# First block ahead, first loads reordered, router logits in four column groups: one order string for another

## The chip, the core and the metric

The kernel runs on one core of one Trainium2 chip. The metric is the device time of one execution in microseconds (us), as a median of runs. A core has a matmul engine (PE, or TensorE, with its weight loads shown apart as PEld), a vector engine (DVE), an activation engine (ACT) and a general-purpose engine (POOL). Each takes its instructions in program order. SP issues most of the DMA transfers, and ACT issues a few at the start. Matmuls write to PSUM, which DVE and ACT then read.

## What is computed

The input x has 4 batches of 1024 tokens with 128 features, all in float32. The work is one pre-norm block, cut here to what matters:

```
xn      = layernorm(x)
Q, K, V = silu(xn @ Wq), silu(xn @ Wk), silu(xn @ Wv)     # 8 heads of 16
scores  = (Q K^T + rel_bias[i - j]) / 4, causal, keys that are all zero masked
attn    = silu(scores) V                                   # silu, not softmax
x       = x + attn * silu(xn @ Wu)
x2      = layernorm(x)
logits  = x2 @ w_gate^T                                    # 8 experts
gates   = softmax over the two largest logits, 0 elsewhere
out     = x + sum_e gates[e] * ((x2 @ w_in[e]^T) @ w_out[e]^T)
```

## The kernel before, in words

**Tiling.** A batch has two blocks of 512 tokens, and a block has four tiles of 128 tokens. `prepare(b, blk)` (L289) makes one block's projections: a layer norm with four transposes onto the PE (L283), a copy to SBUF (L284), K (L304, with ACT writing two half-masked copies of it, one for even and one for odd heads, L307), Q (L312, L313), the key mask (DVE compares the two K copies, L318; four small matmuls, L323; L328), V (L334, L339, and POOL's L341, which writes the masked values `vp`) and U (L351, L352).

**Attention.** `attend` (L355) takes a group of query tiles: groups 0 to 6 are whole blocks, and the last block is split in two groups of two tiles. A group consists of units. A unit is up to 512 score columns for the four heads of one parity. The PE writes them into four PSUM banks (L425), DVE adds the bias from the table `near` (L444) or ACT reads the banks directly where the bias is constant (L452), ACT applies the silu (L447), and one step later the PE weighs the values with the result (L403). When a group is done, DVE multiplies by U (L412) and queues `finish`.

**Router and experts.** `finish` (L470) adds the residual, makes the second layer norm, computes the router logits (L494, copied out by DVE at L496), chooses the top two with a chain of some fifteen small DVE operations and one POOL power (L520), and for groups 0 to 6 sends the gates through DRAM to all partitions (L542 to L547), where DVE multiplies them into the tokens (L553). `experts` (L561) then sums over the experts on the PE (L567). Here w_in and w_out of each expert have been folded into one 128x128 matrix beforehand (`fold`, L242, PE work at L248). The last two groups use `experts_then_gates` (L576): expert products first (L585), gates applied afterwards on ACT (L593) and DVE (L595), then POOL (L599, L600) and DVE (L601).

**What sets the order.** Every one of these functions is a generator that yields between steps, and the string ORDER (L41) says which lane takes its next step: P and Q prepare block 0 and block 1 of each batch, S is one attention unit's scores, W weighs the oldest unit, C, D and E are `finish` of groups 0, 1, 2 modulo 3, X, Y and Z their experts, G the fold, K the constants (the bias table's diagonal and far parts, L193, and clearing `vp`), H the warm-up (L234: four matmuls of the identity with itself, read by nobody). The scheduler doesn't reorder: the letters are the program order of every engine. The string begins:

```
"HHHPPPQQKKKPQPPQQKPQSQKSGGSWSWSG..."
```

All PSUM results except the attention sums share a ring of seven banks (RING, L33, `misc`, L83). A unit takes four of them. So a step waits for the reader of the bank that it reuses.

**First loads.** SP issues x of block 0 and block 1 of batch 0 (L101, L102), the two parities of the bias table `near` (L110), the extended table `ext` to DRAM and from it the two far parts of `near` (L122, L124), then x of batch 1 and the expert weights (L145). ACT issues the bias `rb`, the four projection weights (L107), `cfar` (L131: 1024 elements of 4 bytes) and the gate weights `wgT` (L135).

Of the kernel before, what the change touches and what calls it, by code (L numbers as in the profile page):

```python
# [8 lines left out]
F32 = mybir.dt.float32  # L9
BF16 = mybir.dt.bfloat16  # L10
AF = mybir.ActivationFunctionType
# [5 lines left out]
P = 128  # L17
H = 8
# [5 lines left out]
SB = 512  # L24
TPB = SB // P
E = 8
HID = 512
EPS = 1e-5
NEG = -4294967295.0
# [1 line left out]
OFF = -3.0e38  # L31
EULER = 2.718281828459045
RING = 7  # L33
LAST = 2


# [2 lines left out]


ORDER = (  # L41
    "HHHPPPQQKKKPQPPQQKPQSQKSGGSWSWSGPWPSWWSCPWCSSQWWSCPSQCCPSCWCWPCSCCCWSQGSCWWKCSPPPSWSWSWWCS"
    "WGPSWSWDQSWWSDPGQCWSQQPGQPCCSWSDEQECPPWSQPDSWDWSEGDQEDEDESDWWEDSWQEDSWEWDSXDSWESXSWSWWDSXQ"
    "SEWWSECXECPSWSDEWDWSQPSWDWWDSQYSWWSEEYQPPCSCDSDWCCCESCEWWWCSYQCDSCWSCQYDDCSWWCDWPPQSWSEZQE"
    "SWWSZDCQDSCWDSZCDZCEDDSWDSEEEDWEWSXCSWWCESEWSWSEDDDEXDEXEXDCWDEWSYDCDCCCSCDCCDYCSWDWDCEDDS"
    "CYEYCDSDEEWDWWWDZEEEYYZEZEYEEEEZEYCECCECEEYZYZZZZXZXXX"
)


# [1 line left out]
def preln_silu_attention_moe(  # L51
# [13 lines left out]
    nc = tc.nc  # L65
    B, S, D = x.shape
    NR = rel_biasT.shape[1]
# [15 lines left out]
    def misc():  # L83

        return ps_s.tile([P, SB], F32, tag="bank", name="bank")


    xs = [xpool.tile([P, NT, D], F32, tag="x", name=f"x{b}") for b in range(B)]

# [9 lines left out]
    NPAD = MAXLEN - 1 + TAB  # L99
    FAR = TAB - MAXLEN  # L100
    load_x(0, 0)  # L101
    load_x(0, 1)  # L102
    rb = cpool.tile([H, NPAD], F32, tag="rb", name="rb")
    nc.scalar.dma_start(rb[:, NPAD - NR :], rel_biasT)
    wcat = cpool.tile([P, 4, D], F32, tag="wcat", name="wcat")
    for i, w in ((1, wk), (0, wq), (2, wv), (3, wu)):
        nc.scalar.dma_start(wcat[:, i, :], w)  # L107
    near = cpool.tile([P, 2, NQ, TAB + P], F32, tag="near", name="near")
    for par in range(2):
        nc.sync.dma_start(  # L110
# [3 lines left out]
                [[1, P], [2 * NR, NQ], [1, MAXLEN]],  # L114
            ),
        )
    nc.vector.tensor_copy(
        rb[:, : NPAD - NR], rb[:, NPAD - NR : NPAD - NR + 1].to_broadcast([H, NPAD - NR])
    )
    gates_d = dpool.tile([B * NB, E, SB], F32, tag="gates_d", name="gates_d")  # L120
    ext = dpool.tile([H, NPAD], F32, tag="ext", name="ext")
    nc.sync.dma_start(ext[:, :], rb)  # L122
    for par in range(2):
        nc.sync.dma_start(  # L124
            near[:, par, :, FAR - P : FAR],
            bass.AP(
                ext.tensor, ext.offset + par * NPAD + FAR - P, [[1, P], [2 * NPAD, NQ], [1, P]]
            ),
        )
    cfar = cpool.tile([P, H], F32, tag="cfar", name="cfar")  # L130
    nc.scalar.dma_start(  # L131
        cfar, bass.AP(rel_biasT.tensor, rel_biasT.offset, [[0, P], [NR, H]])
    )
    wgT = cpool.tile([P, E], F32, tag="wgT", name="wgT")
    nc.scalar.dma_start(wgT, w_gateT)  # L135
    experts_in = []
    for e0 in range(0, E, 2):
        if e0 in (0, 4):
            load_x(1, e0 // 4)

        if e0 % 4 == 0:
            room = gpool.tile([P, 2, 2, 2, NC, D], F32, tag="wide", name=f"w_in_out_{e0}")
        both = room[:, e0 // 2 % 2]
        for t, w in zip((both[:, 0], both[:, 1]), (w_in, w_outT)):
            nc.sync.dma_start(t, w[e0 : e0 + 2].rearrange("e (c p) d -> p e c d", p=P))  # L145
        experts_in.append(both)
    for n in range(2 * NB, B * NB):
        load_x(n // NB, n % NB)

    def near_of(k, parts):  # L150

# [81 lines left out]

    def warm():  # L234

        for _ in range(3):
            pt = misc()
            for i in range(TPB):
                nc.tensor.matmul(pt[:, i * P : (i + 1) * P], ident, ident, start=True, stop=True)
            yield  # L240

    def fold():  # L242

        for e0, both in zip(range(0, E, 2), experts_in):
            for e in range(2):
                pt = misc()
                for c in range(NC):
                    nc.tensor.matmul(  # L248
                        pt[:, :D], both[:, 0, e, c, :], both[:, 1, e, c, :],
                        start=(c == 0), stop=(c == NC - 1),  # L250
                    )
                nc.scalar.copy(wfold[:, e0 + e, :], pt[:, :D])
                yield
# [35 lines left out]
    def prepare(b, blk):  # L289

        if b not in batches:
            batches[b] = {
                "qT": bpool.tile([P, S], F32, tag="qT", name=f"qT{b}"),
                "kT": bpool.tile([P, 2, S], F32, tag="kT", name=f"kT{b}"),
                "uT": bpool.tile([P, S], F32, tag="uT", name=f"uT{b}"),
                "vp": vps[b % 2],
            }
        qT, kT, uT, vp = (batches[b][n] for n in ("qT", "kT", "uT", "vp"))
        t0 = blk * TPB
        s0 = blk * SB  # L300
        xnT = spool.tile([P, SB], F32, tag="xnT", name="xnT")
        yield from layernorm_T(xs[b][:, t0 : t0 + TPB, :], xnT, "ACT", (b, blk) == (0, 0))
        pt = misc()
        nc.tensor.matmul(pt, wcat[:, 1, :], xnT, start=True, stop=True)  # L304

        for par in range(2):
            nc.scalar.activation(  # L307
                kT[:, par, s0 : s0 + SB], pt, AF.Silu, scale=sel[:, par : par + 1]
            )
        yield  # L310
        pt = misc()
        nc.tensor.matmul(pt, wcat[:, 0, :], xnT, start=True, stop=True)  # L312
        nc.scalar.activation(qT[:, s0 : s0 + SB], pt, AF.Silu)  # L313
        yield


        nz = spool.tile([P, SB], BF16, tag="nz", name="nz")
        nc.vector.tensor_tensor(  # L318
            nz, kT[:, 0, s0 : s0 + SB], kT[:, 1, s0 : s0 + SB], ALU.not_equal
        )  # L320
        pt = misc()
        for i in range(TPB):
            nc.tensor.matmul(  # L323
                pt[:, i * H : (i + 1) * H], nz[:, i * P : (i + 1) * P], ones8,
                start=True, stop=True,
            )
        kmask = spool.tile([P, TPB, H], F32, tag="kmask", name="kmask")
        nc.vector.tensor_scalar(  # L328
            kmask.rearrange("p i h -> p (i h)"), pt[:, : TPB * H], 0.0, None, ALU.not_equal
        )  # L330
        yield
        pt = misc()
        for i in range(TPB):
            nc.tensor.matmul(  # L334
                pt[:, i * P : (i + 1) * P], xnT[:, i * P : (i + 1) * P], wcat[:, 2, :],
                start=True, stop=True,
            )
        v = spool.tile([P, TPB, D], F32, tag="v", name="v")
        nc.scalar.activation(v.rearrange("p i d -> p (i d)"), pt, AF.Silu)  # L339
        for par in range(2):  # L340
            nc.gpsimd.tensor_tensor(  # L341
                vp[:, t0 : t0 + TPB, par, :, par, :],
                v.rearrange("p i (k q c) -> p i k q c", k=NQ, q=2)[:, :, :, par, :],
                kmask.rearrange("p i (k q) -> p i k q", q=2)[:, :, :, par]
                .unsqueeze(3)
                .to_broadcast([P, TPB, NQ, HD]),
                ALU.mult,
            )
        yield
        pt = misc()  # L350
        nc.tensor.matmul(pt, wcat[:, 3, :], xnT, start=True, stop=True)  # L351
        nc.scalar.activation(uT[:, s0 : s0 + SB], pt, AF.Silu)  # L352
        yield

# [115 lines left out]
    def finish(g, b, t0, nt, gated):  # L470
# [18 lines left out]

        xT = spool.tile([P, nt, P], F32, tag=f"x2T{nt}", name="x2T")  # L490
        yield from layernorm_T(x2, xT.rearrange("p i t -> p (i t)"), "DVE", nt < TPB)
        pt = misc()
        for i in range(nt):
            nc.tensor.matmul(pt[:, i * E : (i + 1) * E], xT[:, i, :], wgT, start=True, stop=True)  # L494
        lg = eight("lg")
        nc.vector.tensor_copy(lg, pt[:, : nt * E].rearrange("p (i e) -> p i e", e=E))  # L496
        yield

        def first_of_largest(v, m, oh, k):
# [61 lines left out]
    def experts(b, t0, gated):  # L561

        y = spool.tile([P, TPB, D], F32, tag="y", name="y")
        for i in range(TPB):
            pt = misc()
            for e in range(E):
                nc.tensor.matmul(  # L567
                    pt[:, :D], gated[:, e, i * P : (i + 1) * P], wfold[:, e, :],
                    start=(e == 0), stop=(e == E - 1),
                )  # L570
            nc.vector.tensor_tensor(y[:, i, :], pt[:, :D], xs[b][:, t0 + i, :], ALU.add)  # L571
            if i == TPB - 1:
                store(b, t0, TPB, y)
            yield

    def experts_then_gates(b, t0, nt, xT, gates):  # L576
# [3 lines left out]
        for i in range(nt):  # L580
            one = xs[b][:, t0 + i, :]
            gy = spool.tile([P, EH, D], F32, tag="gy", name="gy")
            for e0 in (EH, 0):
                pt = misc()
                nc.tensor.matmul(  # L585
                    pt, xT[:, i, :], wfold[:, e0 : e0 + EH, :].rearrange("p e d -> p (e d)"),
                    start=True, stop=True,
                )
                for e in range(EH):
                    ye = pt[:, e * D : (e + 1) * D]  # L590
# [83 lines left out]
```

## Time and profile before

| | us |
|---|---|
| median of three runs | 291.55 (291.19 to 292.44) |
| the profiled execution | 292.34 |
| its span, first to last instruction | 290.2 |
| PE busy / DVE / ACT / POOL | 278.4 / 228.5 / 198.9 / 102.1 |
| first score matmul (L425) starts | 20.96 |
| last expert matmul (L567) ends in the chain of waits | 282.06 |

The span is 2.1 us shorter than the time of the same execution. An engine's busy time is the union of its instructions. Since matmuls are pipelined, and their ends are modelled, a busy PE says only that something was in it. The distance from one matmul's start to the next one's start, which the timeline gives, says more. A float32 matmul stands in the trace as two passes (two instructions), so 32 router matmuls are "x64". A transpose is one pass.

### The profile page before, as it was taken

The numbers are of one execution on the slowest core, as the hardware profiler recorded it, in microseconds if no ns is written. First come the engines' busy times: TensorE is split into PE (matmuls) and PEld (weight loads), VectorE is DVE, ScalarE is ACT, GpSimd is POOL, SyncE is SP. The second block draws the span as 40 slices with busy tenths as digits, with TensorE's granted clock in tenths as the row PEclk, the third lists the DMA queues.
The fourth block names the chain that finished last, engine by engine and source line by source line (L and its number), as shares of the span: only waits on it lengthen the run. The fifth ranks groups of instructions, "written<-read, shape, count | busy, mean of one in ns | idle before, by whom it ended". The sixth has DMA issues, their size and how long they took to land.

```text
span 290.2 us, 6505 instructions
## 1 busy us (share of the span) xinstructions
PE 278.4 (96%) x2591; PEld 161.4 (56%) x2591; DVE 228.5 (79%) x571; ACT 198.9 (69%) x327; POOL 102.1 (35%) x126
## 2 busy tenths in 40 slices
PE   8599999999999999999999999999999999999993
PEld 8255434344445445355653463666676687787873
DVE  4148957688998876879878979887999887797794
ACT  1166899899879779778789787775686683472120
POOL 3913079033306868101125347101601162102251
PEclk9779999999999999999999999999999999999999
DMA  6999100000070000000444300016001702617102
GB/s 190 267 312 317 44 3 1 2 0 3 2 291 0 2 0 3 0 3 0 167 165 145 150 0 0 2 38 273 20 1 40 291 5 75 255 33 296 40 0 72
DMA packets 22061, 25.47 MB, mean 88 GB/s; under 512 B 1952, under 2 KB 21128, under 8 KB 21136
## 3 DMA queue, kind: packets, MB, share of 16 engines
q1 hardware_dynamic: 20256, 24.78, 24.6%
q10 hardware_dynamic: 1776, 0.29, 0.6%
q8 instruction: 20, 0.33, 0.5%
q14 instruction: 9, 0.07, 0.1%
HBM read 22.83 MB, written 2.24 MB: 86 GB/s over the span
## 4 chain that ended last, share of the span: by engine, by line
PE 54%; issue 17%; POOL 17%; DVE 7%; ACT 2%; DMA 1%; POOLq 0%; DVEq 0%
PE bank L425 14%; PE bank L567 14%; PE av L403 12%; POOL xn L276 11%; DVE w L444 5%; POOL rstd L271 4%; PE bank L585 2%; PE bank L494 2%; PE bank L304 2%; PE bank L312 2%; POOL vp L341 2%; PE bank L334 2%; PE bank L283 2%; DMA x<-in_L_attn_x 1%; PE bank L351 1%
## 5 line engine op out<-in xcount | busy, mean ns | idle before, releaser
L444 DVE TENSOR_TENSOR w<-bank,near 128x512 f32<-128x512 f32 (+2 forms) x220 | 116.4, 591 | 22.2 <-PE bank L425 18.7
L447 ACT ACTIVATE w<-w 128x1024 f32<-128x1024 f32 (+2 forms) x110 | 98.4, 913 | 35.7 <-DVE w L444 32.5
L425 PE MATMUL bank<-qT,kT 32*128 32x512 f32 (+3 forms) x864 | 85.6, 481 | 0.0
L452 ACT ACTIVATE w<-bank,cscaled 128x512 f32<-128x512 f32 (+3 forms) x136 | 69.6, 597 | 12.5 <-PE bank L425 12.4
L403 PE MATMUL av<-w,vp 128*32 128x512 f32 (+3 forms) x864 | 71.9, 456 | 0.0
L567 PEld LDWEIGHTS bank<-wfold,gated 128*128 128x128 f32 x448 | 51.9, 192 | 8.1 <-DVE w L444 2.4
L425 PEld LDWEIGHTS bank<-qT,kT 32*128 32x128 f32 x864 | 36.2, 184 | 36.1 <-issue 13.0
L567 PE MATMUL bank<-wfold,gated 128*128 128x128 f32 x448 | 55.1, 279 | 0.0
L276 POOL TENSOR_SCALAR xn<-x,st,rstd 128x128 f32<-128x128 f32 x59 | 52.2, 896 | 1.8
L271 POOL TENSOR_TENSOR rstd<-rs,mhalf 128x4 f32<-128x4 f32 (+1 forms) x17 | 19.0, 1118 | 78.6 <-DVE rs L267 60.5
L403 PEld LDWEIGHTS av<-w,vp 128*32 128x32 f32 x864 | 22.5, 109 | 39.8 <-issue 31.1
L553 DVE TENSOR_TENSOR gated<-gated,x2T 128x1024 f32<-128x1024 f32 x28 | 34.5, 1254 | 0.0
L520 POOL TENSOR_TENSOR ex<-euler,d 128x4 f32<-128x4 f32 (+1 forms) x9 | 10.8, 1199 | 52.8 <-DVE d L518 47.7
L341 POOL TENSOR_TENSOR vp<-v,kmask 128x256 f32<-128x256 f32 x16 | 9.7, 630 | 44.5 <-ACT v L339 44.5
L283 PE MATMUL bank<-ident,xn 128*128 128x128 f32 x64 | 12.8, 299 | 5.8 <-POOL xn L276 5.7
L593 ACT ACTIVATE gy<-bank,gates 128x128 f32<-128x128 f32 x16 | 4.6, 368 | 16.7 <-PE bank L585 10.7
L283 PEld LDWEIGHTS bank<-ident,xn 128*128 128x128 f32 x64 | 8.1, 148 | 11.5 <-POOL xn L276 8.6
L262 DVE BATCH_NORM_STATS2 st<-x 128x6 f32<-128x256 f32 x32 | 12.2, 420 | 0.8 <-DMA x<-in_L_attn_x 0.5
L307 ACT ACTIVATE kT<-bank,sel 128x512 f32<-128x512 f32 x16 | 10.2, 704 | 1.6 <-PE bank L304 1.6
L571 DVE TENSOR_TENSOR y<-bank,x 128x128 f32<-128x128 f32 x28 | 7.8, 284 | 2.9 <-PE bank L567 2.9
L304 PE MATMUL bank<-xnT,wcat 128*128 128x512 f32 x16 | 10.1, 729 | 0.0
L248 PEld LDWEIGHTS bank<-w_in_out 128*128 128x128 f32 x64 | 7.9, 191 | 2.7 <-issue 1.0
(77 smaller groups left out, 211.5 us busy)
## 6 DMA issues: line engine op xcount, KB each, us to landing
gated<-gates_d SPq DMA_DIRECT2D x7, 2048.0 KB, 7.1
x<-in_L_attn_x SPq DMA_DIRECT2D x8, 256.0 KB, 4.2
w_in_out<-in_L_ffn_w_in SPq DMA_DIRECT2D x4, 512.0 KB, 6.2
w_in_out<-in_L_ffn_w_out SPq DMA_DIRECT2D x4, 512.0 KB, 6.3
out<-y SPq DMA_DIRECT2D x7, 256.0 KB, 2.4
near<-in_L_attn_rel_bias SPq DMA_DIRECT2D x2, 512.0 KB, 6.4
near<-ext SPq DMA_DIRECT2D x2, 256.0 KB, 5.3
out<-y SPq DMA_DIRECT2D x2, 128.0 KB, 1.9
```

Of the source, the lines that this page charges most:

```text
L271: nc.gpsimd.tensor_tensor(rstd[:, :nt], rs[:, :nt], mhalf[:, :nt], ALU.pow)
L276: (nc.vector if quick and i != 1 else nc.gpsimd).tensor_scalar(xn[:, i, :], src[:, i, :], st[:, i, 1:2], rstd[:, i : i + 1], ALU.subtract, ...
L283: nc.tensor.transpose(pt[:, i * P : (i + 1) * P], xn[:, i, :], ident)
L304: nc.tensor.matmul(pt, wcat[:, 1, :], xnT, start=True, stop=True)
L341: nc.gpsimd.tensor_tensor(vp[:, t0 : t0 + TPB, par, :, par, :], v.rearrange("p i (k q c) -> p i k q c", k=NQ, q=2)[:, :, :, par, :], kmask ...
L403: nc.tensor.matmul(acc[k * 32 : (k + 1) * 32, nt * P - n : nt * P], vp[:, j, par, k, :, :].rearrange("p q c -> p (q c)"), w[:, k, c : c + ...
L425: nc.tensor.matmul(ps[k][:, c : c + n], kT[k * 32 : (k + 1) * 32, par, j * P : (j + 1) * P], qT[k * 32 : (k + 1) * 32, lo : lo + n], start ...
L444: nc.vector.tensor_tensor(w[:, k, :nn], ps[k][:, :nn], near_of(k, parts), ALU.add)
L447: nc.scalar.activation(w[:, k : k + 2, :nn], w[:, k : k + 2, :nn], AF.Silu, scale=SCALE)
L452: nc.scalar.activation(w[:, k, lo:hi], ps[k][:, lo:hi], AF.Silu, bias=cscaled[:, h : h + 1], scale=SCALE,)
L553: nc.vector.tensor_tensor(wide_g[:, e0 : e0 + 2, :], wide_g[:, e0 : e0 + 2, :], xT.rearrange("p i t -> p (i t)").unsqueeze(1).to_broadcast ...
L567: nc.tensor.matmul(pt[:, :D], gated[:, e, i * P : (i + 1) * P], wfold[:, e, :], start=(e == 0), stop=(e == E - 1),)
```

## The change

The warm-up loop gets a constant HEAT, which is 3 as before, and most PE matmuls go through a helper `product`, so that they all carry its line (L90 in the changed kernel). Beyond that:

- **Order string.** It begins with two steps of block 0, constants, and only then a warm-up step. Block 1's first step comes after the key mask of block 0. The second warm-up step lies further on, among the first scores of batch 1, and the third is the last letter of the string.
- **prepare.** The second K copy is written after Q's copy; before, both came ahead of Q.
- **Loads.** x of block 1 goes behind the first parity of `near`, x of batch 1 block 0 behind the second; `cfar` goes ahead of Wq, Wv and Wu on ACT's queue, and the remaining x loads are spread between the expert weights.
- **Router, groups of four tiles.** `wgT` is padded with zeros from 8 to 32 columns (GW) and becomes the stationary operand. Four matmuls write tile i's logits to partitions 32i to 32i+31, so that each uses one column group of the PE. ACT copies the 128x128 result to SBUF, and one transpose brings it back with tokens on partitions. There is a step boundary between the copy and the transpose. Groups of two tiles keep the old form with 32 columns in place of 8.

```
-    load_x(0, 1)
...
-    for i, w in ((1, wk), (0, wq), (2, wv), (3, wu)):
+    nc.scalar.dma_start(wcat[:, 1, :], wk)
...
+    for i, w in ((0, wq), (2, wv), (3, wu)):
         nc.scalar.dma_start(wcat[:, i, :], w)
+    wgT = cpool.tile([P, GW], F32, tag="wgT", name="wgT")
+    nc.gpsimd.memset(wgT, 0.0)
+    nc.scalar.dma_start(wgT[:, :E], w_gateT)
...
+        load_x(par, 1 - par)
...
+        pk = misc()
+        product(pk, wcat[:, 1, :], xnT)
+        keys(0)
+        yield
+        pt = misc()
+        product(pt, wcat[:, 0, :], xnT)
         nc.scalar.activation(qT[:, s0 : s0 + SB], pt, AF.Silu)
+        keys(1)
         yield
...
+        pt = misc()
+        if nt == TPB:
+            for i in range(nt):
+                nc.tensor.matmul(
+                    pt[i * GW : (i + 1) * GW, :P], wgT, xT[:, i, :], start=True, stop=True
+                )
+            across = spool.tile([P, P], F32, tag="across", name="across")
+            nc.scalar.copy(across, pt[:, :P])
+            yield
+            pt = misc()
+            nc.tensor.transpose(pt[:, :P], across, ident)
+        else:
+            for i in range(nt):
+                product(pt[:, i * GW : (i + 1) * GW], xT[:, i, :], wgT)
         lg = eight("lg")
-        nc.vector.tensor_copy(lg, pt[:, : nt * E].rearrange("p (i e) -> p i e", e=E))
+        nc.vector.tensor_copy(
+            lg, pt[:, : nt * GW].rearrange("p (i e) -> p i e", e=GW)[:, :, :E]
+        )
...
 ORDER = (
-    "HHHPPPQQKKKPQPPQQKPQSQKSGGSWSWSGPWPSWWSCPWCSSQWW...EEEEZEYCEECCECEEYZYZZZZXZXXX"
+    "PPKKPHKKPPQPSPSQPPSWGSQQSWWWPQKSWSCCQWSSWSQKQPPS...ECCECEZCEYEYYZZZZZZXXXXH"
 )
```

## Prediction

> **What bounds the kernel now.** I read the page's shares first, then the chain of waits, then the PE's timeline in the stages that the change touches, and last the view by stretches.
>
> ```profile
> PE 278.4 (96%) x2591; PEld 161.4 (56%) x2591; DVE 228.5 (79%) x571; ACT 198.9 (69%) x327; POOL 102.1 (35%) x126
> ```
> ```profile
> 107.79 0.79 PE bank L494 x8
> 108.58 1.08 PE bank L425 x16
> 109.66 1.85 PE av L403 x16
> 111.51 1.07 PE bank L425 x8
> 112.58 0.59 PE bank L283 x4
> 113.17 0.89 PE bank L248 x8
> ```
>
> PE at 96% alone proves little, since ends are modelled. But in the chain one PE set follows the next without "issue", each at its own price: a unit's scores 1.07, its weighing 0.93 to 1.00, four 128x128 products 0.89. I took the distance between matmul starts through the whole timeline and compared each set with the usual price of its kind. From the first score (20.96) to the end of the last L567 (282.06) only eight places are over by more than 0.12 us. They sum to 4.3 us, and 1.8 of that lies before 60 us. So from 20.96 on the PE is filled with work for 98% of the time. The end moves by the PE's work, by what is lost ahead of 20.96, and by new waits.
>
> ```profile
> 12.68 3.62 PE L304 MATMUL bank<-xnT,wcat 128*128 128x512 f32 x4
> ...
> 20.96 1.14 PE L425 MATMUL bank<-qT,kT 32*128 32x512 f32 x8
> ...
> 22.18 4.28 DVE L444 TENSOR_TENSOR w<-bank,near 128x512 f32<-128x512 f32 x7 [0.67 <-issue]
> ```
>
> These are lines of the opening's timeline (start, length, engine, line). Block 1's transposes wait for POOL's four normalisations (8.71 to 12.36), both K products stand behind those, and DVE gets its first score at 22.18.
>
> **Router, seven groups of four tiles.** Now a group takes 8 passes of 128-column weights for 8 moving columns: 0.79 in the chain, 0.887 as median between starts, so 6.2 us. New is a set of 8 passes with 32-column weights and 128 moving columns in four column groups. The nearest row is L403 with 128 columns (the same form: four column groups): 0.24. The transpose is priced by L542, 0.20 alone (L283 in a row: 0.11). Sum 0.44, saving 7 x 0.44 = 3.1. But there are seven more PE rows, and a weighing set costs 0.88 before its like and 1.00 before another kind, so each break costs about 0.1 to its neighbour; eight more such breaks stand in the new order. I take 2.4 off; bounds 2.0 and 3.4. In the two groups of two tiles 32 moving columns stand in place of 8, but a pass costs 0.112 at 8 columns (L494) as at 128 (L334), so 0. ACT gets seven copies, at most 0.29 each (L252, same shape): 2.0 us on an engine with 69%, hidden unless ACT is late (the second rival). DVE reads the same 32 numbers (L496, 0.185): 0, between -0.1 and +0.3 in all.
>
> **Warm-up steps.** A step is 8 passes: 0.94 at full clock by L334, 1.7 at 0.213 each as L239 ran. The second one now stands among working PE sets: +0.9 (0.86 to 1.0). The third comes after the last L567, where before DVE works on alone from 282.06 to 286.82: 0, or +0.9 without that cover. The PE's work thus changes by -2.4 + 0.9 = -1.5.
>
> **The front, before.** By 20.96 the PE had done 8 transposes (2 x 0.49), two K and two Q (4 x 0.96), the masks (2 x 0.17) and V (2 x 0.99): 7.1 us. Lost: 20.96 - 7.1 = 13.9; with the 1.8 of waits up to 60 us, 15.7.
>
> **The front, after.** x lands at 3.52 as now (first in its queue in both). Statistics, the power and the normalisations end at 6.71 as now. Four transposes, ACT's table load (ends 7.20) and the 0.58 copy give xnT at 8.0 (now 8.3). One warm-up step stands ahead of K: at 0.213 a pass it runs from 7.0 to 8.7 and delays K by 0.7. K and Q at half clock (1.71 each) end at 10.4 and 12.1. ACT writes the first K half, Q and then the second half (0.63 each, after 12.1): 13.6. DVE's comparison (0.69) waits for both halves, and the mask matmuls that wait for it stand ahead of the first scores in the PE's order: 14.3 plus 0.2, first scores at 14.5 (14.0 to 16). The split of the K copies thus brings Q forward and moves the mask back by one copy; the mask is last. Behind it nothing but the first unit is queued on the PE.
>
> By 14.5 the PE has done 0.49 + 2 x 0.96 + 0.17 = 2.6. Lost: 11.9. But block 1's 4.5 us now fall into the first group's attention, where DVE sets the pace: five units of four adds at 0.69 are 13.7 us, with statistics 14.6. The PE has 10 us of attention there, and V, U, K, Q, two sets of transposes and a fold, about 16 in all. That would fill it, if it came in time. Three things are late: the values are ready only at 14.5 + 6.9 (V's silu stands behind two silus of the first unit, then POOL's 1.3 for two L341), so the first weighing waits about 1.3; the third unit waits for banks that the second one's adds free; the last weighing waits for its silu. I count 2.2 us, between 0.5 and 4, and 0.8 for the clock (next part). Together 14.9 against 15.7: -0.8, with ends -4 and +3.
>
> **Loads.** The part of `near` that comes back from `ext` landed at 15 (issued 9.74 and about 10.3, 5.3 to landing). Ahead of it in SP's order, the x load of batch 1 now waits for `cfar`. `cfar`, issued 1.6 earlier, should land near 8.6 (6.8 after issue now), so the issue is near 8.7, the landing near 14; the first add comes at 15.7. The cover is 1.7 us; beyond that each us of delay is one of the end. Wq, behind `cfar`'s 1.21 of issue, lands near 9 by its 5.9; Q starts at 10.4. x of block 1 lands later behind the 512 KB of `near`, but DVE reaches it only after the far table and the 1.76 memset, near 11.6. The extra POOL memset (0.1) precedes the identity, which nobody needs before 6: 0. The fold weights follow near 17 and are first read near 22: 0, or what they are late.
>
> **The clock.** In the view by stretches PEclk is the last column but two:
>
> ```profile
> 5.00:10.00 5.00, 3.01 (x14) 2.50 (x13) 1.75 (x6) 2.07 (x3) 3.85 (x5) 1.00 0.99 258
> 10.00:15.00 5.00, 3.39 (x6) 1.58 (x7) 1.04 (x3) 0.95 (x2) 4.80 (x8) 0.59 1.03 277
> 15.00:20.00 5.00, 5.00 (x23) 2.31 (x22) 1.93 (x5) 3.36 (x6) 0.38 (x2) 0.73 1.05 311
> 20.00:25.00 5.00, 5.00 (x39) 2.69 (x38) 4.33 (x6) 2.55 (x4) 2.55 (x6) 1.00 1.03 306
> ```
>
> The warm-up from 1.4 to 6.9 bought little: in the idle stretch after it the clock fell to half, and all of K and most of Q ran at half until about 17.5. [...] By the row, two warm-up steps fewer cost 0, as K and Q ran at half anyway, and lifting took about 5 us of dense work (12.5 to 17.5); PE work from 7.0 to 12.1 is just that long, and the 2 us wait for the mask follows. [...] I take +0.8.
>
> **The tail.** After the last router logits the PE had 11.1 us left, in the new order 12.9; the gates chain to the last store is the same DVE work, about 15.6 from the logits. DVE ends 4.8 after the PE now, and would end some 3.3 after it. Against it, the last gates transpose (L542) stands 21.4 us before the PE's end rather than 23.4; the copy, two transfers (1.4 and 7.1) and four L553 (1.25 each) need 14 of them, with DVE's next work behind. I take -0.8, between -1.5 and +1.
>
> **Sum.** -1.5 - 0.8 - 0.8 = -3.1 on the profiled span of 290.2, so 287.1, and with the same 2.1 around it 289.2 for that execution of 292.34. That one lies 0.8 over the median of 291.55, so in medians 288.4.
>
> **Rivals.**
> *The start pays in full.* If block 1's work fits between the first units with as few waits as the 0.2 that 21 to 32 us shows now, and the clock is up by the first score, the front is worth 11.9 + 0.5 - 15.7 = -3.3 rather than -0.8: 288.4 - 2.5 = 285.9. For it: work of many lanes lies ready. Against it: V isn't there yet. 0.15.
> *The round trip through ACT: slower.* The router path now goes PE, ACT, PE. A transposing matmul that waits for its copy holds every later PE set. Between logits and transpose the new order has 2.2 us (group 0), 3.0, 3.7, 4.4, 3.9, 6.4 and 3.0 of PE work, and ACT must reach its copy within that, behind silus of 1.06 and direct reads of 0.69. From 40 to 60 us ACT is busy 18.0 of 20; a unit's backlog is 2.8. It decides from a wait of 0.44 us per group on (3.1 / 7). At a wait of 1.0: 7.0 - 3.1 = +3.9, thus 295.4. Against it: ACT idles 35.7 us for DVE and 12.4 for the PE now, so it is mostly early. 0.23.
> *The start gives nothing.* The clock is still low at the first score (+1.7 more) or the far table lands 1 to 2 us late; the front turns from -0.8 to +1.5: 290.7. What the router saves is then given back. 0.20.
>
> **How the numbers follow.** The forecast, 288.4, has 0.42, with its own range 286.9 to 290.2. A measurement here tells 0.5% (1.5 us) from no change. Faster (under 290.1): the first rival's 0.15, 0.39 of the forecast's 0.42, and 0.06 of the last rival: 0.60. Same: 0.03 and 0.13, and 0.02 of a short round trip: 0.18. Slower: the round trip's other 0.21 and 0.01 of the last rival: 0.22. For 8 in 10 the range goes from 285.0, which takes in most of the first rival, to 294.5, which takes in the round trip up to some three quarters of its price.
>
> **What would show it.** First score matmul near 14.5 and first add near 15.7; a router set of 0.24 and a transpose of 0.2 or less in the chain; L510 without idle time ahead of it "<-ACT across". PE starts over their price up to 60 us: about 2 to 3 us. Wrong if L510 waits, if PEclk is 0.5 beyond 15 us, if an add waits for `near<-ext`, or if other PE sets after 60 us wait more than the 2.5 us of now, which no view of before can show of a new order.

## The result, and the profile after

| | before | after |
|---|---|---|
| median of eight runs each, side by side | 291.43 us | 289.01 us |
| lowest and highest run | 290.93 to 292.44 | 286.89 to 290.6 |
| the profiled execution, and its span | 292.34, 290.2 | 289.95, 287.9 |

The ratio is 0.9913 (0.9893 to 0.9933): 2.4 us, or 0.9%, faster. The forecast was 288.4 and faster, in a range of 285.0 to 294.5. So the number held. The parts of its sum did not, as the runs below show.

The page's rows of engine totals (busy time, share of the span, instructions) and of the granted clock (tenths, 40 slices of 7.2 us), for the changed kernel:

```profile
PE 274.2 (95%) x2598; PEld 157.3 (55%) x2598; DVE 227.3 (79%) x571; ACT 198.5 (69%) x334; POOL 98.7 (34%) x127
PEclk9959999999999999999999999999999999999999
```

PE's busy time fell by 4.2, the span by 2.3. The clock row has a 5 in its third slice, where before had two 7s. The opening's timeline tells more (start, length, engine, line; in brackets the idle time ahead and what ended it):

```profile
6.86 0.38 SPq L124 DMA_DIRECT2D near<-in_L_attn_rel_bias  x1
6.89 0.38 ACTq L119 DMA_DIRECT2D wgT<-in_L_ffn_w_gate  x1
...
7.30 1.28 ACT L184 ACT_TABLE_LOAD   x1 [7.30 <-POOL xn L284]
...
8.70 0.57 ACT L292 COPY xnT<-bank 128x512 f32<-128x512 f32 x1
...
9.45 2.70 PE L90 MATMUL bank<-xnT,wcat 128*128 128x512 f32 x4
...
11.32 0.69 ACT L313 ACTIVATE kT<-bank,sel 128x512 f32<-128x512 f32 x1 [2.06 <-PE bank L90]
...
12.68 0.68 ACT L313 ACTIVATE kT<-bank,sel 128x512 f32<-128x512 f32 x1
12.84 0.64 POOL L206 TENSOR_SCALAR_AFFINE_SELECT near<-near 128x512 f32<-128x512 f32 x1 [4.57 <-DMA near<-in_L_attn_rel_bias]
13.39 0.69 DVE L329 TENSOR_TENSOR nz<-kT 128x512 bf16<-128x512 f32 x1 [1.47 <-ACT kT L313]
...
14.93 0.19 POOL L225 TENSOR_SCALAR_AFFINE_SELECT ones<-ones 128x8 bf16<-128x8 bf16 x1
...
15.17 0.25 PE L90 MATMUL bank<-ones,nz 128*128 128x8 bf16 x4 [3.03 <-POOL ones L225]
...
15.35 2.09 PE L432 MATMUL bank<-qT,kT 32*128 32x512 f32 x8
...
17.52 0.69 DVE L451 TENSOR_TENSOR w<-bank,near 128x512 f32<-128x512 f32 x1 [1.86 <-PE bank L432]
```

First scores start at 15.35, not 20.96, but also not at the predicted 14.5. The comparison of the K copies is on time, at 14.08 rather than 14.3, but partly by luck. ACT's table load, which the prediction let end at 7.20, starts only at 7.30, behind the issue of the gate weights on ACT's queue. So xnT is ready at 9.27 rather than 8.0, and the first K copy starts at 11.32, where K was to be done at 10.4. Q then runs at full clock and makes up for it: it ends near 12.1, as forecast. The mask matmuls wait until 15.17 for `ones`, a constant. POOL builds it in the same lane K, after both parities' diagonals in `near`, and the second parity's transfer landed at 12.78. The set of eight score passes then takes 2.09 where 1.07 is its price, because the clock is at half, as the view by stretches has it (the clock is the last column but two):

```profile
5.00:10.00 5.00, 3.43 (x13) 2.96 (x14) 2.54 (x8) 1.96 (x3) 3.10 (x4) 1.00 0.91 190
10.00:15.00 5.00, 2.15 (x4) 0.62 (x3) 2.58 (x5) 1.86 (x3) 1.95 (x5) 0.95 0.99 249
15.00:20.00 5.00, 4.83 (x32) 3.08 (x35) 2.67 (x5) 1.06 (x1) 4.27 (x6) 0.50 1.08 287
20.00:25.00 5.00, 5.00 (x33) 1.82 (x30) 3.42 (x9) 3.54 (x4) 1.25 (x3) 0.87 1.13 291
```

The clock's record says half from 14.46 to 21.29 here, and from 10.88 to 17.71 before: 6.8 us each time, but here under work that the end depends on. The chain of waits shows the new router (start, length, what):

```profile
55.51 0.22 PE bank L503 x8
55.73 0.86 PE av L410 x16
56.59 1.07 PE bank L432 x8
57.66 0.19 PE bank L90 x4
57.85 0.17 PE bank L510
58.02 0.89 PE bank L90 x8
```

A set of logits costs 0.22 here (0.25 on average over the seven), its transpose 0.17 (between starts 0.109 as median, 0.14 on average), and nothing stands between "PE bank L90" and L510: no wait for ACT.

**Where the 2.3 us of span come from.** I summed the distances between matmul starts by kind, from the first score matmul to the last product (L567, now under L90), in both traces; waits are in the kind that they follow. "Block 1's work" is at the price that its kinds have in before. "Predicted" splits the front's -0.8 by its own working; its +1.2 is the 2.2 and 0.8 less the 1.8 of before.

| term | measured | predicted |
|---|---|---|
| first scores earlier | -5.6 | -6.5 |
| block 1's work, now behind them | +4.6 | +4.5 |
| router rows (7.02 to 3.60) | -3.4 | -2.4 |
| warm-up step in the middle | +1.1 | +0.9 |
| transposes (14.69 to 11.87), less the 0.5 that moved in | -3.3 | 0 |
| values and scores: half clock and waits | +4.2 | +1.2 |
| all other kinds together | -0.1 | 0 |
| from the start of PE's last product to the end (4.9 to 5.1) | +0.2 | -0.8 |
| sum (the span itself: -2.3) | -2.3 | -3.1 |

The fifth line was not in my account: in before, the transposes of later blocks waited for POOL's normalisations, as its waits show from 26 to 283 us (total, times, longest). After has no such entry. By the distances, seven transposes of before took over 0.25, and three of these waits stood in one set at 101 us; after has two such, both short.

```profile
PE bank L283 <- POOL xn L276: 2.1, 5, 0.4
```

### The profile page after: what moved, and what is told of

Its sections match the earlier page's. It is cut to its first block, busy times and chain, and to the rows that moved or that the text cites. A ratio compares the mean times of both kernels' runs of the same rounds, so it can differ in the third digit from the quotient of the medians.

```text
span 287.9 us, 6529 instructions
## 1 busy us (share of the span) xinstructions
PE 274.2 (95%) x2598; PEld 157.3 (55%) x2598; DVE 227.3 (79%) x571; ACT 198.5 (69%) x334; POOL 98.7 (34%) x127
## 4 chain that ended last, share of the span: by engine, by line
PE 85%; DMA 4%; POOL 3%; DVE 3%; ACT 2%; issue 1%; SPq 0%; DVEq 0%; POOLq 0%; ACTq 0%
PE bank L90 32%; PE bank L432 27%; PE av L410 21%; DMA near<-in_L_attn_rel_bias 4%; PE bank L291 3%; POOL xn L284 1%; PE bank L481 1%; ACT w L459 1%; DVE y L615 1%; DVE w L451 1%; POOL rstd L279 1%; PE bank L503 1%; POOL vp L348 0%; ACT w L454 0%; DVE gated L574 0%
## 5 line engine op out<-in xcount | busy, mean ns | idle before, releaser
L432 PE MATMUL bank<-qT,kT 32*128 32x512 f32 (+3 forms) x864 | 88.8, 490 | 0.0
L432 PEld LDWEIGHTS bank<-qT,kT 32*128 32x128 f32 x864 | 37.8, 187 | 37.7 <-issue 12.7
L90 PEld LDWEIGHTS bank<-wfold,gated 128*128 128x128 f32 x448 | 51.9, 192 | 6.2 <-issue 1.6
L90 PE MATMUL bank<-wfold,gated 128*128 128x128 f32 x448 | 54.8, 278 | 0.0
L284 POOL TENSOR_SCALAR xn<-x,st,rstd 128x128 f32<-128x128 f32 x59 | 48.9, 842 | 1.7
L574 DVE TENSOR_TENSOR gated<-gated,x2T 128x1024 f32<-128x1024 f32 x28 | 33.8, 1221 | 0.0
L541 POOL TENSOR_TENSOR ex<-euler,d 128x4 f32<-128x4 f32 (+1 forms) x9 | 9.9, 1097 | 65.5 <-DVE d L539 56.6
L90 PE MATMUL bank<-xnT,wcat 128*128 128x512 f32 x48 | 24.9, 628 | 0.0
L291 PE MATMUL bank<-ident,xn 128*128 128x128 f32 x64 | 11.4, 293 | 6.6 <-DVE xn L284 6.5
L90 PEld LDWEIGHTS bank<-xnT,wcat 128*128 128x128 f32 x48 | 8.2, 198 | 9.2 <-issue 3.6
L270 DVE BATCH_NORM_STATS2 st<-x 128x6 f32<-128x256 f32 x32 | 12.1, 418 | 0.7 <-DMA x<-in_L_attn_x 0.6
L313 ACT ACTIVATE kT<-bank,sel 128x512 f32<-128x512 f32 x16 | 11.1, 696 | 2.1 <-PE bank L90 2.1
L90 PEld LDWEIGHTS bank<-w_in_out 128*128 128x128 f32 x64 | 7.8, 191 | 4.0 <-DVE rs L275 0.8
```

The source lines that it names most:

```text
L90: nc.tensor.matmul(out, stationary, moving, start=start, stop=stop)
L270: nc.vector.bn_stats(st[:, i : i + 2, :].rearrange("p i s -> p (i s)"), pair if nt > 1 else pair.to_broadcast([P, D, 2]),)
L284: (nc.vector if quick and i != 1 else nc.gpsimd).tensor_scalar(xn[:, i, :], src[:, i, :], st[:, i, 1:2], rstd[:, i : i + 1], ALU.subtract, ...
L291: nc.tensor.transpose(pt[:, i * P : (i + 1) * P], xn[:, i, :], ident)
L313: nc.scalar.activation(kT[:, par, s0 : s0 + SB], pk, AF.Silu, scale=sel[:, par : par + 1])
L432: nc.tensor.matmul(ps[k][:, c : c + n], kT[k * 32 : (k + 1) * 32, par, j * P : (j + 1) * P], qT[k * 32 : (k + 1) * 32, lo : lo + n], start ...
```

## The experiments

All were run in five rounds beside the kernel before. Where nothing else is said, the edit is to the changed kernel. The kernel before had medians of 291.7 (first four), 292.1 (next four) and 291.9 (last three). The table above has 291.4 for it, so differences between kernels of different rounds carry up to 0.7 from the rounds alone; the ratios to before do not.

**1. Everything but the router.** The old form of the logits, with the step boundary kept:

```
         if nt == TPB:
-            for i in range(nt):
-                nc.tensor.matmul(
-                    pt[i * GW : (i + 1) * GW, :P], wgT, xT[:, i, :], start=True, stop=True
-                )
...
+        for i in range(nt):
+            product(pt[:, i * E : (i + 1) * E], xT[:, i, :], wgT[:, :E])
+        if nt == TPB:
             yield
```

> The changed kernel with the old router matmuls (tokens' transposes as weights, 8 moving columns, no copy on ACT, no transpose back) and an empty step where the copy was, so that every other letter stays in its place. Theory (the PE is filled, the router's saving is on the path): it takes 3.4 us more than the changed kernel, about 292.4, which is slower than before by 1. Rival (the gain is the earlier start, the router's PE time is slack): within 1 us of the changed kernel, 289 to 290.

Measured: 293.94 (293.24 to 295.49), ratio 1.008 (1.0056 to 1.0103). It is 4.9 over the changed kernel. So without the router the change makes the kernel slower, by 2.2 us, and the router is worth twice what I gave it. In the trace the router rows are 7.67 against 3.60 and the weighing sets 69.14 against 68.34, which makes up the 4.9. The 0.1 that I charged for each break to its neighbour didn't come; the weighing sets are cheaper beside the new form. Nearly all of that 0.8 (0.7) lies in the six places where a weighing set stands right ahead of the logits: its last pass takes 0.52 to the next start there with the old form, 0.41 with the new, which has 32-column weights like the weighing itself.

**2. The router alone, in the kernel before**, with copy and transpose in one step:

```
+            across = spool.tile([P, P], F32, tag="across", name="across")
+            nc.scalar.copy(across, pt[:, :P])
+            pt = misc()
+            nc.tensor.transpose(pt[:, :P], across, ident)
```

> The kernel before with the new router alone, copy and transpose in one step, so that nothing is placed between the column-group matmuls and the transpose that waits for ACT. Theory: seven times 0.56 less PE work (3.9), but seven bare round trips of about 0.2 + 0.3 + 0.2 plus what ACT has queued (0.5 on average): +7 x 1.2 = 8.4, so about 296, slower by 1.5%; L510's counterpart idles for ACT's copy. Rival (ACT is early and the round trip is cheap anywhere): -3.9 + 7 x 0.5 = about 291, no change.

Measured: 308.87 (307.05 to 310.07; a sixth execution, 311.75 and 1.5% over the fastest, is left out), ratio 1.0563 (1.0526 to 1.06): some 17 us slower, far over the expected 296. One of its seven groups, from its timeline:

```profile
51.45 2.19 ACT L449 ACTIVATE w<-w 128x1024 f32<-128x1024 f32 x2 [0.16 <-DVE w L446]
51.49 0.43 PE L497 MATMUL bank<-x2T,wgT 128*32 128x128 f32 x8
53.54 0.57 ACT L286 COPY xnT<-bank 128x512 f32<-128x512 f32 x1
54.01 0.27 ACT L501 COPY across<-bank 128x128 f32<-128x128 f32 x1
54.33 0.33 PE L503 MATMUL bank<-ident,across 128*128 128x128 f32 x1 [2.42 <-ACT across L501]
```

The logits are done before 52, but ACT has two silus and a copy in front of `across`, and PE stands for 2.42 us with every later set behind the transpose. The groups by line give the total (busy, mean ns, idle ahead, what ended it):

```profile
L503 PE MATMUL bank<-ident,across 128*128 128x128 f32 x7 | 2.3, 328 | 13.2 <-ACT across L501 13.2
```

13.2 us in seven waits. By the distances between starts the router takes 18.49 there, against 7.02 in before, the weighing 3.8 more and the scores 2.0 more. In the changed kernel the same row, L510, has none: two to six us of other PE work stand between the two halves there. Part of the 3.8 and 2.0 comes from the clock, which falls to half for 3.4 us in four more places, from 54.9, 184.6, 205.1 and 239.2 us; in the 3.4 us before each of them the PE was busy for 1.0 to 1.8 us only. The first of them, which follows the wait shown above:

```profile
51.46:54.88 3.42, 1.00 (x11) 0.52 (x11) 1.27 (x3) 2.74 (x4) 0.00 (x0) 1.00 0.00 0
54.88:58.30 3.42, 3.42 (x14) 0.72 (x16) 1.75 (x8) 0.78 (x2) 0.00 (x0) 0.50 0.02 5
```

So where the two halves stand decides whether the column groups pay. The two kernels differ in the whole order string, though; the changed kernel with only its step boundary taken out was not tried.

**3 to 5. The constant and the clock.** Kernel 3 builds `ones8` before the diagonals:

```
+        nc.gpsimd.memset(ones8, 1.0)
...
         for par in range(2):
...
-        nc.gpsimd.memset(ones8, 1.0)
```

> The changed kernel with the small mask matrix `ones8` built by POOL ahead of the bias table's diagonals rather than behind them. Theory (first scores wait for POOL's ones8, which stands behind the wait for the second parity of `near`): mask matmuls go at 14.1 and the first scores at 14.3 rather than 15.35, and the time falls by about 1 us to 288.0. Rival (DVE's adds or the half clock set the first stage): first scores earlier, but the time unchanged at 289.0.

Kernel 4 moves the middle and the last warm-up step into the gap ahead of the first scores:

```
-    "PPKKPHKKPPQPSPSQ...SPCGWSHCW"
+    "PPKKPHKKPPHHQPSPSQ...SPCGWSCW"
...
-    "...ZZZZZZXXXXH"
+    "...ZZZZZZXXXX"
```

> The changed kernel with its second and third warm-up steps moved to the front, between Q and the mask matmuls of the first block, where the PE stood idle from 12.1 to 15.2. Theory (the idle gap drops the clock to half from 14.5 to 21.3, and the warm-up step among the scores of batch 1 costs 0.94 of PE time): no stretch at half clock after 12 us, 2.9 less in the executions that had it and the 0.94 less in all, so about 286 with little spread. Rival (in that stage the PE waits for DVE and ACT anyway): only the 0.94, 288.1. Second rival (the gap isn't what drops the clock): PEclk 0.5 from 14.5 on as before.

Kernel 5 has both edits:

> Both edits of the last two experiments in one: the mask matrix built ahead of the bias table, and two warm-up steps between Q and the mask. Theory (the wait for ones8 and the half clock are separate losses): first scores near 14.4 instead of 15.83 with the gap filled alone, no stretch at half clock after 12.2, so 1.2 less than the 287.2 of the filled gap: 286.0. Rival (the two overlap, since the adds of DVE set the first stage): 287.0.

Measured: 287.62 (286.51 to 288.65), 287.19 (286.81 to 288.02) and 286.4 (286.22 to 286.46), that is 1.4, 1.8 and 2.6 under the changed kernel; ratios to before 0.9851 (0.9825 to 0.9877), 0.9844 (0.9823 to 0.9864) and 0.9807 (0.9793 to 0.9821), against 0.9913 for the changed kernel, which makes 1.8, 2.0 and 3.1. Stretches from 15 us on, kernel 3 and then kernel 4:

```profile
15.00:20.00 5.00, 5.00 (x37) 3.01 (x30) 3.07 (x5) 2.24 (x3) 3.80 (x5) 0.68 1.09 288
```
```profile
15.00:20.00 5.00, 4.34 (x40) 2.65 (x40) 3.15 (x6) 1.49 (x2) 4.62 (x9) 1.00 1.16 290
```

In kernel 3 first scores come at 14.42, the comparison is the last input as predicted, and the half clock lasts 3.4 us rather than 6.8. In kernel 4 they come at 15.83, half a us later than in the changed kernel, and still it is faster, as the clock is never at half after 12.2 in its profiled execution. So `ones` and the clock are both real. With the clock full, `ones` early brings the first scores from 15.83 to 14.69 and is worth 0.8 (kernel 5 against kernel 4). Which of the two is the larger, and how far they overlap, the noise does not tell; kernels 4 and 5 also lack the warm-up step in the middle (experiment 9). Nor did either reach what was expected of it, 286 and 286.0.

The changed kernel's spread of 3.7 us goes in large part with the clock: in its eight executions the mean clock runs from 0.988 to 0.997 and the span from 288.5 to 285.0. By that mean the clock was at half for some 7 us in the longest execution and 1.7 us (0.003 x 285 x 2) in the shortest, where it may all lie at the end: in kernel 8, with a mean of 0.998, the clock falls at 282.4, 0.9 us before the end. Kernel 5 spreads over 0.24 us in four executions. But kernel 10, with a clock as full, spreads over 2.0 us in fourteen, so the clock isn't all of it.

**6. The load order.** The changed kernel with the load section of before:

```
+    load_x(0, 1)
...
-    nc.scalar.dma_start(wcat[:, 1, :], wk)
...
-    for i, w in ((0, wq), (2, wv), (3, wu)):
+    for i, w in ((1, wk), (0, wq), (2, wv), (3, wu)):
...
-            nc.sync.dma_start(ext[:, :], rb)
...
-        load_x(par, 1 - par)
```

> The changed kernel with the first loads in the order of the kernel before. Theory (the new order moved a wait rather than removed one: the second parity of `near` lands at 12.8 instead of about 10, ones8 and ACT's table load come late for it, while `cfar` lands at 8.1 instead of 10.2): ones8 ready near 12, xnT near 8.3, but DVE behind `cfar` until about 13.9; first scores between 14.5 and 15.2, time within 1 us of the changed kernel, 288.0 to 290.0. Rival (the load order carries the gain of the front): first scores or first adds at 17 or later, 291 or more.

Measured: 288.96 (287.79 to 290.51), ratio 0.99 (0.9869 to 0.9932): no difference from the changed kernel. Its opening shows why:

```profile
10.39 1.20 DVE L210 COPY near<-cfar 128x512 f32<-128x512 f32 x2 [3.42 <-DMA cfar<-in_L_attn_rel_bias]
```
```profile
15.67 0.26 PE L90 MATMUL bank<-ones,nz 128*128 128x8 bf16 x4 [2.77 <-DVE nz L327]
```

With the old order `ones` is ready at 12.65 and xnT at 8.47, but `cfar` comes late. DVE's comparison stands behind the copies of `cfar`, the 1.76 memset and block 1's statistics, starts at 14.93, and first scores come at 15.86 rather than 15.35. One late input replaced another.

**7 and 8. How far the front goes.** Kernel 7 is kernel 5 with three warm-up steps at the head again (HEAT is the number of steps); kernel 8 moves, beyond that, the gate weights' load from ACT's queue to the end of SP's first loads:

```
-HEAT = 3
+HEAT = 5
...
-    "PPKKPHKKPPQPSPSQ..."
+    "HHHPPKKPKKPPHHQPSPSQ..."
...
-    nc.scalar.dma_start(wgT[:, :E], w_gateT)
...
+    nc.sync.dma_start(wgT[:, :E], w_gateT)
```

> As with both edits, but with three warm-up steps ahead of the first transposes, as the kernel before has them, instead of one behind them (five in all, with the two between Q and the mask). Theory (PE busy from 1.5 lifts the clock by about 7.5, and the stretch stays busy): K and Q at full clock end near 10.9 rather than 12.2, first scores near 13, but the first add waits for the part of `near` that comes back from `ext`, which lands near 15.5: first add 15.5 to 15.7, time 0.3 to 1 less than with both edits, 285.0 to 285.7. Rival (a dense stretch so early drops the clock again before the scores): half clock somewhere between 11 and 18, time 1 to 2 more than with both edits.

> As the previous one, with the gate weights' load moved from ACT's queue, where it held ACT's table load until 7.3, to the end of SP's loads. Theory: table load ends at 6.7 rather than 8.6, xnT near 8.0 rather than 9.3, K 1.2 earlier; but the first add still waits for the far part of `near`, so the time gains 0 to 0.5. Rival (xnT sets the front): 1.2 less than the previous one.

Measured: 285.79 (285.76 to 285.91), ratio 0.9788 (0.9774 to 0.9801), and 285.37 (285.14 to 285.44), ratio 0.9771 (0.9757 to 0.9785). Kernel 7 missed its 13 for the first scores: the clock fell again, from 8.6 to 12.0, K and Q ran at half, and first scores came at 14.47; it is 0.6 under kernel 5 all the same. Kernel 8 is the fastest of all: 2.3% under before and some 3.6 us under the changed kernel (4.1 by the ratios). Its timeline:

```profile
8.06 1.98 PE L90 MATMUL bank<-xnT,wcat 128*128 128x512 f32 x4 [0.67 <-ACT xnT L292]
...
12.90 0.25 PE L90 MATMUL bank<-ones,nz 128*128 128x8 bf16 x4 [1.08 <-DVE nz L329]
13.09 1.14 PE L432 MATMUL bank<-qT,kT 32*128 32x512 f32 x8
...
15.13 4.87 DVE L451 TENSOR_TENSOR w<-bank,near 128x512 f32<-128x512 f32 x8 [1.75 <-POOL rstd L279]
```

ACT's table load no longer waits behind an issue on ACT's own queue: it starts at 5.37, not at 6.48 as in kernel 7, where the issue ran from 6.12 to 6.45, or at 7.30 as in the changed kernel. K and Q take 1.98 for the four passes, full clock. First scores come at 13.09. But DVE's first add comes at 15.13, 2 us after them. The row names POOL; the last input to land was the table's far part `near<-ext`, at 15.01, so I read the wait as one for that transfer. It is the place where the prediction's "beyond that each us of delay is one of the end" would now hold; that was not tried by another load order.

**9. The middle warm-up step.** Only that letter taken out:

```
-    "...SPCGWSHCW"
+    "...SPCGWSCW"
```

> The changed kernel without the warm-up step among the first scores of batch 1; the last letter of the string then makes the second step and nothing makes the third. Theory (the PE is filled there): 0.9 less, 288.1. Rival (the step lies in a gap that DVE leaves): 289.0 as the changed kernel. The clock in the front is untouched, so the spread stays as wide as the changed kernel's.

Measured: 289.14 (288.63 to 289.38), ratio 0.991 (0.9893 to 0.9927). By the medians nothing was gained, where 0.9 was expected; the spread, expected as wide as before, was 0.75. The changed kernel at this place, and then the one without the step:

```profile
77.10 1.17 PE L432 MATMUL bank<-qT,kT 32*128 32x512 f32 x8
78.20 1.16 PE L90 MATMUL bank<-ident 128*128 128x128 f32 x8
79.29 1.06 PE L410 MATMUL av<-w,vp 128*32 128x512 f32 x8
```
```profile
76.40 1.17 PE L432 MATMUL bank<-qT,kT 32*128 32x512 f32 x8
78.05 1.07 PE L410 MATMUL av<-w,vp 128*32 128x512 f32 x8 [0.48 <-DVE attended L419]
```

From the scores' start to the weighing's it is 2.19 with the step and 1.65 without, so about half of the step's 1.09 returns as a wait for DVE. The other half, 0.54, is within what the changed kernel's own runs scatter. It may well be real: four executions each had a mean clock of 0.988, with medians of 289.85 (changed kernel) and 289.24 (this one), and the kernel before was 0.5 slower in this one's rounds. So the step fills half of a hole that the order has there, and what it costs beyond that, between 0 and 0.9, these runs don't settle.

**10. Front mended, old router.** Kernel 5 with the edit of kernel 1:

> Both edits (mask matrix ahead, two warm-up steps in the gap) on the changed kernel with the old router. Theory (the router is worth 4.9 wherever the PE is filled): 286.4 + 4.9 = 291.3, so first block alone, loads and the new string, even with clock and wait mended, only break even with the kernel before. Rival (the old router had lost so much only because of the half clock): 289 to 290, a gain of the front by itself.

Measured: 291.34 (290.61 to 292.62), ratio 0.9988 (0.9974 to 1.0002). As expected, to the tenth: with full clock and early `ones`, the new order and loads break even with before. The router is worth 4.9 here as well (286.4 against 291.34, from different rounds; 5.3 by the ratios).

**11. Both K copies ahead of Q's**, in kernel 8:

```
         keys(0)
+        keys(1)
...
-        keys(1)
```

> The fastest so far (gate weights on SP, three warm-up steps first) with both K copies ahead of Q's copy again, as the kernel before had them. Theory: the mask comes 0.6 earlier and the first scores with it, 12.5 rather than 13.1, but the first add still waits for the far part of `near` at 15.1: no change, 285.4. Rival (the mask, and so the place of the second K copy, sets the front): 0.6 less, 284.8.

Measured: 285.45 (285.11 to 285.65), ratio 0.9783 (0.9765 to 0.9801): no change, as expected. But the first scores, expected at 12.5, moved from 13.09 to 13.57: in both kernels DVE's comparison stood behind its memset and statistics, not behind the K copies (in kernel 8 the second copy ends at 11.25 and the comparison starts at 12.16), and here `cfar` landed 0.6 later. Even so

```profile
15.09 2.48 DVE L451 TENSOR_TENSOR w<-bank,near 128x512 f32<-128x512 f32 x4 [1.23 <-DMA near<-ext]
```

the first add stays where it was, now with the transfer named (landed at 14.97). So what the first scores gain or lose here is covered by that wait, and this run supports the reading of the row in kernel 8. What the split of the K copies costs by itself it does not show.

## Why the prediction was right or wrong

The number was right by luck, because two errors cancelled: the router was worth 2.5 us more than forecast, everything else 2.9 us less (+2.2 in kernel 1 against -0.7).

- **Router, -2.4: mis-sized, measured -4.9.** A set costs 0.25 on average, as priced by L403 (0.24). The transpose, taken at the 0.20 of a transpose standing alone, costs 0.14 on average. The breaks at 0.1 each had the wrong sign: the weighing gained 0.8. And the old form costs more in the new order than in the old (7.67 against 7.02), so that its rows saved 4.1.
- **Round trip through ACT (the slower rival, 0.23): the mechanism is real, but not in this order.** L510 waits for nothing in the changed kernel. In kernel 2, without the step boundary, the wait is 1.9 us per group on average, far over the deciding 0.44.
- **Front, -0.8: wrong in two of its steps.** "The mask is last" and 14.5 for the first scores: the comparison came as worked out, to 0.3 us, but only because xnT, 1.3 late behind the table load, and Q at full clock cancelled. The moved work of 4.5 us was right. Of a step that moves, every instruction counts, and I had followed lane K's loads and DVE's part of it, not POOL's part, which builds `ones` behind the second parity of `near`. Kernel 3 takes this away: 1.4 us, part of it through the clock. The other step is the next point. Scores and values lost 4.2 to half clock and waits, where 1.2 was in the sum.
- **The clock, +0.8: mis-sized, about 2** (1.8 in kernel 4; in its trace scores and values take 2.2 less than in the changed kernel's). No run shows the 0.8, which was my estimate; the runs show 6.8 us at half clock from 14.46 on, under the first scores, and the 1.8 of kernel 4. "Two warm-up steps fewer cost 0" rested on the row in which K and Q ran at half anyway. But in the changed kernel PE was busy for 1.10 us only of the 3.41 from 11.05 to 14.46, and then the clock fell to half; in kernel 4, with two warm-up steps in that gap, it was never at half after 12.2. The cost is not that K and Q run at half but that the clock fell after the gap before the mask, just when the scores begin. The rival "the start gives nothing" (0.20, 290.7; its +1.7 is half of the 5 us that the row shows from 12.5 to 17.5, less the 0.8) named a low clock at the first scores, and it is what happened, only that the router's larger saving covered it.
- **Loads: a cover of 1.7 us, from a landing near 14.** The table's transfer landed at 15.44, 1.4 late. It did no harm, as the add at 17.52 waited for scores; with scores at 14.5 the cover would have been some 0.3. The old load order costs the same (kernel 6). The limit shows only at 15.0, in kernels 8 and 11.
- **Middle warm-up, +0.9: open.** The row is there (1.09), but about half of it returns as a wait for DVE when it goes, and the medians show no gain (kernel 9).
- **Tail, -0.8: wrong sign, +0.2.** I had read 282.06, where the chain leaves PE, as the end of L567, and the table of the profile before has it so. The timeline of before shows otherwise:

```profile
278.13 7.50 PE L567 MATMUL bank<-wfold,gated 128*128 128x128 f32 x64
```

  These are 64 passes, the last of which starts at 285.36. I had taken passes for matmuls in a place that I warned of elsewhere. From that start to the end of the span it was therefore 4.9 and not 8, and became 5.1.
- **Later waits "the 2.5 us of now": too pessimistic.** They fell, by the POOL waits shown above. With the old load section (kernel 6) the transposes still have it, 11.86, and with the old router (kernel 1) too, 11.77. So the new string is what is left, with the split of the K copies.

What stays open: with the clock full, scores still cost 2.0 us more than before (82.54 in kernel 5 against 80.56). About 0.55 of that is the wait for DVE at 75 us that kernel 9 shows too; no run takes the rest apart. Whether the shared 32-column form is what makes the weighing cheaper ahead of the new logits was not tried alone either.

## What to carry to other kernels

When an order is made anew, list for the first instruction that all wait on every input, constants included, with the engine that makes it and what stands ahead of it there. Ask of each idle stretch on the PE not only what it costs but what comes right after it, since that is what ran at half clock here (eight score passes in 2.09 us rather than 1.07): two spare steps moved into the gap gave 1.8 here (one of them left a place where it cost up to 0.9), while three in place of one at the start gave 0.6 on top. A product that comes back through another engine was cheap here only with other work put between its two halves: the same edit was worth -4.9 us in an order that puts such work there, and some +17 in one without.

## What the hardware showed beyond that

In these traces the clock stayed at half for 3.4 us (kernel 3) or for twice that, 6.8 (changed kernel and before), and in one kernel with three warm-up steps at its head it still fell, from 8.6 to 12.0 (kernel 7); with PE starting K 0.45 us sooner (kernel 8) it did not. Cut by 3.41 us from the start of each trace's clock record, PE's busy time sorts these cases. The changed kernel, and then kernel 3 (PE busy is the second number, the clock again the last but two):

```profile
11.05:14.46 3.41, 1.10 (x3) 0.29 (x2) 1.53 (x5) 1.86 (x3) 1.55 (x2) 1.00 0.97 275
14.46:17.88 3.42, 2.71 (x14) 1.18 (x14) 0.56 (x2) 0.00 (x0) 3.18 (x8) 0.50 1.10 285
17.88:21.29 3.41, 3.41 (x24) 2.22 (x22) 2.12 (x4) 2.31 (x3) 1.50 (x2) 0.50 1.05 288
```
```profile
11.34:14.75 3.41, 1.36 (x10) 0.48 (x12) 1.86 (x6) 1.75 (x3) 1.69 (x3) 1.00 1.03 265
14.75:18.16 3.41, 3.41 (x16) 1.78 (x8) 1.86 (x4) 0.54 (x1) 3.31 (x5) 0.50 1.13 289
```

In all thirteen traces the half clock ended after stretches in which the PE was busy throughout (twelve), and went on after the four with 2.4 to 2.7 us. The full clock fell only after stretches with 2.0 us or less; between 1.6 and 2.0 us it sometimes held (before had 1.68 from 283.95 to 287.36 and kept it, kernel 7 had 1.96 and lost it, kernel 8 had 2.54 and kept it). Matmul ends are modelled, so these bounds are rough, and I can't say from these runs what sets the phase.

A set of four float32 products of 128x128 by 32 columns, in four column groups, takes 0.22 us at best, that is 0.027 a pass, against 0.11 a pass where the whole width is used (L494 of before): passes of different column groups start 0.007 apart (L503, each 0.27 long), so the four groups ran beside each other. And a load's issue held up its engine's own work: with the gate weights issued on ACT's queue at 6.89 the table load began at 7.30 (changed kernel), with the issue at 6.12 at 6.48 (kernel 7), and with that one issue moved to SP at 5.37 (kernel 8).
